# Routed experts: token rows scattered to their slots from SBUF and loaded back plainly, instead of stored in order and gathered

## The chip, the cores and the metric

The kernel runs on one core of one Trainium2 chip. A core has a matrix engine (TensorE, PE in the profile; PEld is its weight load), a vector engine (VectorE, DVE), a scalar engine (ScalarE, ACT), GpSimd (POOL) and SyncE (SP), which here only issues DMAs. The engines run their own instruction streams and wait for one another on semaphores. The metric is device time in microseconds (us), the median of several runs; lower is better.

## The reference, cut to what matters

The network takes x of shape (2, 1024, 128), two batches of 1024 tokens with 128 features, and has two blocks. The first (a recurrence and six layers of windowed attention with a gated feed-forward) is not touched by the change. The second is an attention with 16 heads over all tokens of a batch, and then a mixture of experts:

```python
h = _layernorm(x, axis=-1) * (1 + ca) + sa
x = x + ga * _L1_attn_ref(h, ...)                 # 16 heads of 64, relative bias, softmax
h = _layernorm(x, axis=-1) * (1 + cb) + sb
x = x + gb * _L1_ffn_ref(h, ...)

def _L1_ffn_ref(x, gate_w, w1, b1, w2, b2):       # E = 8 experts, F = 512
    router_logits = xf @ gate_w
    top_vals, top_idx = jax.lax.top_k(router_logits, 2)
    top_w = jax.nn.softmax(top_vals, axis=-1)
    onehot = jax.nn.one_hot(top_idx, E, dtype=xf.dtype)
    cw = jnp.einsum('tk,tke->te', top_w, onehot)
    out = jnp.zeros_like(xf)
    for e in range(E):
        h = jax.nn.gelu(xf @ w1[e] + b1[e], approximate=False)
        out = out + cw[:, e:e + 1] * (h @ w2[e] + b2[e])
```

Each token goes through two of the eight experts. Which two depends on the data, so the kernel sorts the 2048 (token, expert) pairs of a batch by expert on the chip and computes only those.

## The kernel before, in words

The second block starts at about 1650 us. Its attention (`attention`, L1283) runs over 128 tiles: 2 batches, 8 pairs of heads, 8 tiles of 128 queries. In each tile PE makes the scores (L1393), DVE their maxima (L1409), ACT the exponentials (L1419), DVE the reciprocal of their sum (L1422), and POOL scales the two probability tiles (L1423, "ap"). Two tiles later PE transposes them (L1432), ACT and DVE copy the transposes out of PSUM (L1435), and three tiles later PE multiplies them with the values (L1445). At tile 3 and 5 of each eight, PE makes the next pair's queries and keys (L1338, tiles "aq" and "ak") and values (L1359), SP loads two relative-bias tiles ("abias", L1377), and POOL subtracts their first column (L1381). The order of PE, DVE and ACT is the order in which the code calls them (`manual_schedule`); POOL's and SP's orders are left to a scheduler that works with its own estimates of time.

All the work on routing is cut into small pieces, kept in a list; after each tile one piece is taken from it (`next_piece`, L1279). When half a batch's attention is done (a segment of 512 tokens), `expert_tokens` (L1577) appends the pieces of its layer norm (`norm_pieces`), which centres the tokens (tile "ln_xc") and stores them in order to DRAM ("centred", L1496), and of its routing. When a batch is complete, `dispatch` (L1640) sorts its pairs. `summed` and `counted` make ranks by matmuls with a triangle of ones; `placed` gives each pair its slot (tile "slot": token by token, first and second choice) and each row its expert. A row is 128 slots that all have the same expert; there are ROWS = 2*8+8-1 = 23 rows a batch, 2944 slots, of which 2048 are filled. `split`, `hot0`, `hot1` and `listed` (32 matmuls, L1745) turn the map round, from slot to pair, and `numbered` makes of it "tokens" (which token a slot reads) and "homes" (where its result goes). Then `slots_gathered` (L1935) gathers each row's 128 tokens from "centred" with one indirect DMA on POOL, 23 a batch: for batch 0 within the attention of batch 1 (`first_rows`, two rows a piece), for batch 1 within the expert stage.

The expert stage (`experts`, L1857) runs 46 rows, one a step of a loop over n, with steps of different rows overlapped: `row_weights` (the row's expert is read into a register of SP, and 514 KB of weights are loaded, "row_w", L1954; 8 buffers, asked for up to 8 rows ahead, the first two rows' in the attention already), `row_features` of row n (PE turns the row, L1960, DVE scales it, L1962), `row_hidden` of row n-2 (8 matmul instructions, L1973, and four gelu on ACT, L1977), and `row_outputs` of row n-4 (8 matmul instructions, L1989, a product on DVE, "row_y", L1997, 12 buffers, and an indirect DMA on POOL that scatters the 128 results to "outputs" in DRAM, L1998). The late half of batch 1 (its last segment's layer norm and routing) has no attention left to lie beside: `late_steps` (L1888) hangs its parts on certain steps, `placed` and `split` on step 9, `numbered` on 13; from step 13 on one gather of batch 1 follows each step. From step 36 on the pairs of batch 0 are loaded ("pair_y", L2018; SP waits for all their scatters) and summed (L2034). Here PE, DVE, ACT and SP have a hand-made order, POOL the scheduler's.

Of the kernel before, what the change touches and what calls it, by code (L numbers as in the profile page):

```python
# [57 lines left out]

GATHER = 13
# [39 lines left out]
class Net:  # L99
# [1149 lines left out]
    def second_block(self):  # L1249
# [5 lines left out]
        engines = {ET.PE, ET.DVE, ET.Activation}  # L1255
        with ExitStack() as es:
# [7 lines left out]
            with ExitStack() as at:  # L1264
# [3 lines left out]
                with tc.manual_schedule(engines=engines):  # L1268
                    self.attention(work)
# [13 lines left out]
    def attention(self, work):  # L1283
# [10 lines left out]
        for n in range(len(tiles) + 3):  # L1294
# [75 lines left out]
    def relative_bias(self, head):  # L1370
# [91 lines left out]
    def norm_pieces(self, src, out, scale, bias, b, keep=None, home=None):  # L1462
# [16 lines left out]
        def centred():  # L1479
# [15 lines left out]
            if home is not None:  # L1495
                nc.sync.dma_start(out=home, in_=xc)  # L1496
# [32 lines left out]
    def dispatch_tables(self):  # L1529
# [43 lines left out]
        self.centred_rows = [home(f"centred{b}", [N, D]) for b in range(B)]  # L1573
        self.puts = [[], []]
        self.pair_rows = [home(f"outputs{b}", [2 * N + ROWS * 128, D]) for b in range(B)]

    def expert_tokens(self, seg):  # L1577
# [6 lines left out]
        rows = self.centred_rows[b][i * SEG : (i + 1) * SEG].rearrange("(i p) d -> p i d", p=128)  # L1584
# [5 lines left out]
        if seg == NSEG - 1:  # L1590
            self.late = self.late_norm(self.x3, h, b, tokens, rows), route
            return
        self.norm_pieces(self.x3, h, 4, 3, b, keep=tokens, home=rows)
# [10 lines left out]
    def late_norm(self, src, out, b, tokens, rows):  # L1604
# [19 lines left out]
        def centred():  # L1624
# [7 lines left out]
            nc.sync.dma_start(out=rows, in_=xc)  # L1632
# [7 lines left out]
    def dispatch(self, b):  # L1640
# [28 lines left out]
        def placed():  # L1669
# [28 lines left out]
            nc.vector.tensor_tensor(slot[:, 0], slot[:, 0], slot[:, 1], ALU.subtract)  # L1698
            end = get([128, E], "end")
# [12 lines left out]
            st["expert"] = expert  # L1712

# [39 lines left out]
        def numbered():  # L1753
            ps = st["list"][:, :ROWS]
            pair = get([128, ROWS], "pairs")
            nc.vector.tensor_scalar(pair, ps, -1.0, 0.0, ALU.add, ALU.max)
            second = get([128, ROWS], "second")
            nc.vector.tensor_scalar(second, pair, float(N), float(N), ALU.is_ge, ALU.mult)
            tokens = get([128, ROWS], f"tokens{b}", mybir.dt.uint32)
            nc.vector.tensor_tensor(tokens, pair, second, ALU.subtract)  # L1760
# [4 lines left out]
            self.plan[b] = st["expert"], tokens, homes  # L1765

        def shared():
# [14 lines left out]
            placed=placed,  # L1782
            split=split,
# [73 lines left out]
    def experts(self, work):  # L1857
# [11 lines left out]
        for n in range(len(order) + 4):  # L1869
            while loads < min(len(order), n + 8) and order[loads][0] in self.plan:  # L1870
# [17 lines left out]
    def late_steps(self, work, norm, route, slots):  # L1888
# [39 lines left out]
    def first_rows(self, j0):  # L1928

        for j in range(j0, min(j0 + 2, ROWS)):  # L1930
            self.gathered[0, j] = self.slots_gathered(self.disp, 0, j)
            if j < 2:
                self.early[j] = self.row_weights(self.disp, 0, j, 2)

    def slots_gathered(self, work, b, j, bufs=ROWS):  # L1935
# [208 lines left out]
```

## Time and profile before

| | us |
|---|---|
| median of 3 runs (2742.39 to 2746.73) | 2744.52 |
| the profiled execution, its own time | 2759.36 |
| its span, first to last instruction | 2757.6 |
| first block, until about | 1650 |
| attention of the second block | 1670 to 2602 |
| expert stage with its sums | 2602 to 2757 |

| stretch, us | PE busy | POOL busy | granted clock | GB/s of DMA |
|---|---|---|---|---|
| 2362.25 to 2415.30 (eight attention tiles) | 52.39 of 53.05 | 19.36 | 1.00 | 9 |
| 2285.24 to 2362.25 (eight tiles with batch 0's gathers) | 62.57 of 77.01 | 43.52 | 0.89 | 26 |
| 2652.15 to 2700.21 (rows 16 to 26) | 34.84 of 48.06 | 30.28 | 0.75 | 169 |
| 2700.21 to 2726.53 (rows 27 to 39) | 26.32 of 26.32 | 13.08 | 1.00 | 287 |

How to read the profile: a line of the timeline gives the start, the busy time, the engine, the line of the kernel, the operation, the tile written and the tiles read ("out<-in"), and how many instructions are merged; in brackets stands the idle time before it and what released it. "issue" there means that the engine waited for nothing that the profile shows, "remote" that the releaser could not be told. SPq is SP's issuing of a DMA, not its transfer. The ends of matmuls are modelled from their starts, so a busy PE need not be a PE at its peak. The granted clock is the share of the full clock that PE was given. For DMA_INDIRECT the time shown is the time that POOL takes to issue it.

### The profile page before, as it was taken

The page shows a single profiled execution, that of the slowest core. Times are in us where ns is not written, and L with a number is a line of the kernel's source. Part 1 is how long each engine was busy: PE and PEld are TensorE (multiplying, and loading weights), DVE is VectorE, ACT ScalarE, POOL GpSimd, SP SyncE. Part 2 cuts the span into 40 slices and gives each one's busy share as a digit, 9 for nine tenths or more (in the row PEclk, how much of TensorE's full clock was granted, in tenths as well). Part 3 has the DMA queues.
Part 4 walks back from the last instruction along what each step waited for, and adds up shares of the span by engine and source line. Part 5 has one row for each costly group of instructions (what it writes and reads, how often), then busy time and mean ns, then how long its engine had stood idle before and what let it go on. Part 6 is the DMA issues. An engine that isn't in the chain of part 4 may idle for free. (4 is left out here: it accounts for less than half of the span.)

```text
span 2757.6 us, 67119 instructions
## 1 busy us (share of the span) xinstructions
PE 2573.7 (93%) x29054; PEld 1735.0 (63%) x29054; DVE 1947.2 (71%) x2744; ACT 1726.1 (63%) x2562; POOL 1673.5 (61%) x1312
## 2 busy tenths in 40 slices
PE   7899999999999999999999989999999998999977
PEld 4466666666666666666666655666666665666676
DVE  6788788888878887878778845666665665666434
ACT  5467777777777777777777765555554553555424
POOL 3687888888888878887878733333332335333154
PEclk9999999999999999999999999999999999999979
DMA  7000100000010001000000010000000001000256
GB/s 193 4 2 2 32 2 9 25 10 2 9 32 2 7 4 32 2 9 2 2 2 2 2 43 18 7 7 11 9 7 11 11 7 43 8 1 1 74 165 219
DMA packets 44051, 71.02 MB, mean 26 GB/s; under 512 B 5511, under 2 KB 32269, under 8 KB 42733
## 3 DMA queue, kind: packets, MB, share of 16 engines
q1 hardware_dynamic: 40156, 59.24, 7.2%
q0 software_dynamic: 3168, 6.89, 0.9%
q8 instruction: 229, 3.75, 0.6%
q10 hardware_dynamic: 432, 0.61, 0.1%
q14 instruction: 66, 0.53, 0.1%
HBM read 61.56 MB, written 9.36 MB: 26 GB/s over the span
## 5 line engine op out<-in xcount | busy, mean ns | idle before, releaser
L1423 POOL TENSOR_SCALAR ap<-ap,a_den 128x1024 f32<-128x1024 f32 x256 | 287.0, 1134 | 557.7 <-DVE a_den L1422 557.6
L993 POOL TENSOR_TENSOR qk<-qk,turned 128x1024 f32<-128x1024 f32 x192 | 453.8, 2363 | 194.3 <-DVE turned L982 187.0
L1419 ACT ACTIVATE ap<-two,a_neg 128x1024 f32<-128x1024 f32 x256 | 285.4, 1115 | 295.7 <-DVE a_neg L1409 294.5
L1409 DVE TENSOR_REDUCE a_neg<-two 128x1 f32<-128x1024 f32 x256 | 301.2, 1218 | 175.9 <-PE two L1393 163.2
L1131 PEld LDWEIGHTS two<-px,wvo 128*128 128x128 f32 x3072 | 356.4, 192 | 56.8 <-issue 29.3
L956 PE MATMUL proj<-wqk,xs 128*128 128x512 f32 x764 | 370.4, 607 | 22.7 <-DVE turned L982 21.6
L1131 PE MATMUL two<-px,wvo 128*128 128x128 f32 x3072 | 361.6, 276 | 17.5 <-ACT xw L1093 17.2
L1005 POOL TENSOR_TENSOR qk<-qk,w_inv 128x1024 f32<-128x1024 f32 x192 | 361.6, 1904 | 3.9 <-ACT w_inv L1002 2.8
L1432 PEld LDWEIGHTS two<-fixed,ap 128*128 128x128 f32 x2048 | 223.1, 142 | 139.7 <-issue 121.2
L1432 PE MATMUL two<-fixed,ap 128*128 128x128 f32 x2048 | 277.3, 279 | 16.9 <-ACT ap L1419 14.1
L967 ACT ACTIVATE sq<-proj 128x1024 f32<-128x1024 f32 x191 | 195.9, 1026 | 133.7 <-PE proj L956 133.0
L1445 PE MATMUL two<-apT,av 128*64 128x128 f32 x4096 | 257.5, 279 | 15.5 <-ACT apT L1435 11.6
L975 DVE TENSOR_TENSOR qk<-proj,rot 128x1024 f32<-128x1024 f32 x191 | 232.6, 1218 | 49.1 <-ACT sq L967 43.4
L1393 PE MATMUL two<-ak,aq 64*128 64x512 f32 x1024 | 259.7, 615 | 4.7 <-DVE gates L1527 1.6
L1445 PEld LDWEIGHTS two<-apT,av 128*64 128x64 f32 x4096 | 225.4, 139 | 37.7 <-issue 21.3
L1079 POOL TENSOR_TENSOR p<-p,w_den 128x1024 f32<-128x1024 f32 x96 | 183.4, 1911 | 98.0 <-DVE ya L1141 86.0
L1121 ACT COPY px<-two 128x1024 f32<-128x1024 f32 x192 | 195.0, 1017 | 76.3 <-PE two L1112 76.3
L1027 PEld LDWEIGHTS two<-fixed,qk 128*128 128x128 f32 x1536 | 165.2, 141 | 111.1 <-issue 82.1
L982 DVE TENSOR_TENSOR turned<-proj,rot 128x1024 f32<-128x1024 f32 x191 | 231.9, 1214 | 1.5 <-POOL qk L993 1.5
L956 PEld LDWEIGHTS proj<-wqk,xs 128*128 128x128 f32 x764 | 133.0, 191 | 147.7 <-issue 110.7
L1027 PE MATMUL two<-fixed,qk 128*128 128x128 f32 x1536 | 204.4, 277 | 20.6 <-ACT px L1121 13.0
L990 DVE TENSOR_REDUCE w_ss<-sq 128x16 f32<-128x1024 f32 x192 | 221.3, 1192 | 1.5 <-ACT sq L967 1.5
(359 smaller groups left out, 4262.6 us busy)
## 6 DMA issues: line engine op xcount, KB each, us to landing
row_w<-expert_rows SPq DMA_DIRECT2D x46, 514.0 KB
wqk<-in_wqkv SPq DMA_DIRECT2D x6, 1024.0 KB
abias<-rel_turned SPq DMA_DIRECT2D x32, 192.0 KB
wv<-in_wqkv SPq DMA_DIRECT2D x6, 512.0 KB
wo<-in_wo SPq DMA_DIRECT2D x6, 512.0 KB
expert_rows<-in_ew SPq DMA_DIRECT2D x1, 2048.0 KB
expert_rows<-in_ew SPq DMA_DIRECT2D x8, 256.0 KB
pair_y<-outputs SPq DMA_DIRECT2D x16, 128.0 KB
```

The source lines that it names most:

```text
L956: self.nc.tensor.matmul(ps[:, g], x.step.xs[:, c0 : c0 + 128], x.step.weights[:, a, g * 512 : (g + 1) * 512], start=True, stop=True,)
L975: nc.vector.tensor_tensor(dst, ps.rearrange("p a (h d) -> p (a h) d", d=DH), cos.unsqueeze(1).to_broadcast([128, H, DH]), ALU.mult,)
L993: self.nc.gpsimd.tensor_tensor(x.qk[a], x.qk[a], x.turned.rearrange("p h e d -> p h (e d)"), ALU.add)
L1005: engine.tensor_tensor(x.qk[a], x.qk[a], x.inv[:, a].unsqueeze(2).to_broadcast([128, H, DH]), ALU.mult)
L1027: nc.tensor.transpose(ps[:, c // 4, c % 4 * 128 : (c % 4 + 1) * 128], flat[:, c * 128 : (c + 1) * 128], self.ident,)
L1131: nc.tensor.matmul(x.out[:, 0, :128].rearrange("p (b q) -> p b q", q=BLK), merged[:, c // 4, par, c % 4], x.px[:, :, h], start=(h == 0), s ...
L1393: nc.tensor.matmul(scores[par][:, j], q[r, tok], k[r, j * 512 : (j + 1) * 512], start=True, stop=True)
L1409: self.nc.vector.tensor_reduce(neg, ps, AX.XY, ALU.max, negate=True)
L1419: nc.scalar.activation(p, ps.rearrange("p a b -> p (a b)"), AF.Exp, bias=neg, accum_out=den)
L1423: nc.gpsimd.tensor_scalar(p, p, den, 1.0, ALU.mult, ALU.mult)
L1432: self.nc.tensor.transpose(ps[:, j // 4, j % 4 * 128 : (j % 4 + 1) * 128], p[:, j * 128 : (j + 1) * 128], self.ident)
L1445: nc.tensor.matmul(ops[r, :128], v[:, j, r], pT[par][:, j], start=(j == 0), stop=(j == NKT - 1))
```

## The change

The centred tokens are no longer stored in order. They stay in SBUF (`self.centred`), and once `placed` has given each pair its slot (copied to integers, "index"), POOL scatters them from there to "slot_rows" in DRAM, where a batch's 2944 slots lie in order: `sent(i)` is one indirect DMA of 128 tokens, 16 a batch, for the two choices of 8 tiles of tokens. For batch 0 they are 16 pieces, one after each attention tile; for batch 1 all 16 stand at step 9 of the expert stage. The slots that no pair fills must hold something finite, so both "slot_rows" are filled with zeros at the start of the second block, by one memset of 128x2944 on POOL and two stores.

The rows are then read with plain loads on SP (`rows_loaded`): all 23 of batch 0 in one, after the last piece of its `dispatch`; those of batch 1 in two, 6 and 17 rows, at step 21. A load waits for all sends of its batch, but the sends don't wait for one another (`put`, `after`). The three operations that made "tokens" in `numbered` go. `split` to `numbered` of batch 1 move from steps 9 to 13 to steps 11 to 15. POOL joins the engines whose order in the attention is given by hand; the subtraction of the bias columns, which its loader called so far, gets a place of its own (`biases_less`: after tile 1 for the first pair, after tile 6 of each eight for the next). "row_w" has 10 buffers instead of 8 and is asked for 6 rows ahead instead of 8, "row_y" 24 instead of 12.

```diff
-                with tc.manual_schedule(engines=engines):
+                with tc.manual_schedule(engines=engines | {ET.Pool}):
                     self.attention(work)
...
+            if n == 1:
+                self.biases_less(qk[0, 0])
+            if n < len(tiles) and t == 6 and n + NKT - t < len(tiles):
+                self.biases_less(qk[tiles[n + NKT - t][:2]])
...
-        r = self.get(self.att, [128, 3 * 128], "abiasr", bufs=4)
-        nc.gpsimd.tensor_tensor(r, t, t[:, 0:1].to_broadcast([128, 384]), ALU.subtract)
-        return r
+        return t
+
+    def biases_less(self, qk):
+        for i, t in enumerate(qk[2]):
+            r = self.get(self.att, [128, 3 * 128], "abiasr", bufs=4)
+            self.nc.gpsimd.tensor_tensor(r, t, t[:, 0:1].to_broadcast([128, 384]), ALU.subtract)
+            qk[2][i] = r
...
-                nc.sync.dma_start(out=home, in_=xc)
+                self.centred[home] = xc
...
-        self.centred_rows = [home(f"centred{b}", [N, D]) for b in range(B)]
-        self.puts = [[], []]
+        self.slot_rows = [home(f"slot_rows{b}", [ROWS * 128, D]) for b in range(B)]
+        zeros = self.disp.tile([128, ROWS, D], F32, tag="slots0_0", name="zeros", bufs=1)
+        nc.gpsimd.memset(zeros, 0.0)
+        for rows in self.slot_rows:
+            nc.sync.dma_start(
+                out=rows.rearrange("(j p) d -> p j d", p=128),
+                in_=zeros,
+            )
+        self.puts, self.sends, self.centred = [[], []], [[], []], {}
...
-            order = "summed counted placed split hot0 hot1 listed numbered shared".split()
-            self.pieces += [steps[k] for k in order]
-            self.pieces += [lambda j=j: self.first_rows(j) for j in range(0, ROWS, 2)]
+            self.pieces += [steps[k] for k in ("summed", "counted", "placed")]
+            self.pieces += [lambda i=i: steps["sent"](i) for i in range(2 * NKT)]
+            self.pieces += [steps[k] for k in "split hot0 hot1 listed numbered shared".split()]
+            self.pieces.append(self.first_rows)
...
-            nc.sync.dma_start(out=rows, in_=xc)
+            self.centred[b, PER_B - 1] = xc
...
+            index = st["index"] = get([128, 2, NKT], f"index{b}", mybir.dt.uint32)
+            nc.vector.tensor_copy(index, slot)
...
+        def sent(i):
+            c, t = i % 2, i // 2
+            put = nc.gpsimd.indirect_dma_start(
+                self.slot_rows[b],
+                bass.IndirectOffsetOnAxis(st["index"][:, c, t : t + 1], axis=0),
+                self.centred[b, t // TT][:, t % TT],
+                None,
+            )
+            self.put(self.sends[b], put)
...
-            while loads < min(len(order), n + 8) and order[loads][0] in self.plan:
+            while loads < min(len(order), n + 6) and order[loads][0] in self.plan:
...
-            j = n - GATHER
-            if 0 <= j < ROWS:
-                gathered[1, j] = self.slots_gathered(self.rows, 1, j, 20)
...
-        at(9, slots["placed"], slots["split"])
-        at(10, slots["hot0"])
-        at(11, slots["hot1"])
-        at(12, slots["listed"])
-        at(13, slots["numbered"])
+        at(9, slots["placed"], *(lambda i=i: slots["sent"](i) for i in range(2 * NKT)))
+        at(11, slots["split"])
+        at(12, slots["hot0"])
+        at(13, slots["hot1"])
+        at(14, slots["listed"])
+        at(15, slots["numbered"])
+        at(21, lambda: self.rows_loaded(work, 1, 0, 6), lambda: self.rows_loaded(work, 1, 6, ROWS))
...
-        x = self.get(work, [128, D], "slots", bufs=bufs)
-        self.nc.gpsimd.indirect_dma_start(
-            x, None, self.centred_rows[b], bass.IndirectOffsetOnAxis(self.plan[b][1][:, j : j + 1], axis=0)
-        )
-        return x
-
-    def row_weights(self, work, b, j, bufs=8):
+    def rows_loaded(self, pool, b, j0, j1):
+        self.n += 1
+        x = pool.tile([128, j1 - j0, D], F32, tag=f"slots{b}_{j0}", name=f"slots{self.n}", bufs=1)
+        rows = self.slot_rows[b][j0 * 128 : j1 * 128].rearrange("(j p) d -> p j d", p=128)
+        self.after(self.nc.sync.dma_start(out=x, in_=rows), self.sends[b])
+        for j in range(j0, j1):
+            self.gathered[b, j] = x[:, j - j0]
+
+    def put(self, earlier, put):
+        for other in earlier:
+            self.tc.declare_no_dep(put.ins, other.ins, reason="their places differ")
+        earlier.append(put)
+
+    def row_weights(self, work, b, j, bufs=10):
...
-        y = self.get(work, [128, D], "row_y", bufs=12)
+        y = self.get(work, [128, D], "row_y", bufs=24)
```

More of the change, by code (lines that the diff above doesn't have):

```diff
@@ L57 @@
 EW = 2 * F1 + F1 // 128
-GATHER = 13
 C_MG, C_MR, C_MK, C_MV, C_BG, C_BR, C_BK, C_BV, C_BO, C_W, C_U = range(11)
@@ L1583, in expert_tokens @@
         h = self.get(self.moe, [128, SEG], "mh", bufs=1)
-        rows = self.centred_rows[b][i * SEG : (i + 1) * SEG].rearrange("(i p) d -> p i d", p=128)
         if i == 0:
@@ L1590, in expert_tokens @@
         if seg == NSEG - 1:
-            self.late = self.late_norm(self.x3, h, b, tokens, rows), route
+            self.late = self.late_norm(self.x3, h, b, tokens), route
             return
-        self.norm_pieces(self.x3, h, 4, 3, b, keep=tokens, home=rows)
+        self.norm_pieces(self.x3, h, 4, 3, b, keep=tokens, home=(b, i))
         self.pieces += [route[k] for k in ("logits", "exponentials", "chosen", "weights")]
@@ L1599, in expert_tokens, with late_norm @@
             steps = self.dispatch(b)
-            order = "summed counted placed split hot0 hot1 listed numbered shared".split()
-            self.pieces += [steps[k] for k in order]
-            self.pieces += [lambda j=j: self.first_rows(j) for j in range(0, ROWS, 2)]
-    def late_norm(self, src, out, b, tokens, rows):
+            self.pieces += [steps[k] for k in ("summed", "counted", "placed")]
+            self.pieces += [lambda i=i: steps["sent"](i) for i in range(2 * NKT)]
+            self.pieces += [steps[k] for k in "split hot0 hot1 listed numbered shared".split()]
+            self.pieces.append(self.first_rows)
+    def late_norm(self, src, out, b, tokens):
         nc, mod, st = self.nc, self.mod1, {}
@@ L1754, in numbered @@
             ps = st["list"][:, :ROWS]
[L1755 to L1760, printed above, removed]
             spare = get([128, ROWS], "spares")
@@ L1764, in numbered @@
             nc.vector.scalar_tensor_tensor(homes, ps, -1.0, spare, ALU.add, ALU.add)
-            self.plan[b] = st["expert"], tokens, homes
+            self.plan[b] = st["expert"], homes
         def shared():
@@ L1782, in dispatch @@
             placed=placed,
+            sent=sent,
             split=split,
@@ L1926, in late_steps, with first_rows, after @@
         return steps
[L1928 to L1935, printed above, removed]
-        x = self.get(work, [128, D], "slots", bufs=bufs)
-        self.nc.gpsimd.indirect_dma_start(
-            x, None, self.centred_rows[b], bass.IndirectOffsetOnAxis(self.plan[b][1][:, j : j + 1], axis=0)
-        )
-        return x
-    def row_weights(self, work, b, j, bufs=8):
+    def first_rows(self):
+        self.rows_loaded(self.disp, 0, 0, ROWS)
+        for j in range(2):
+            self.early[j] = self.row_weights(self.disp, 0, j, 2)
+    def rows_loaded(self, pool, b, j0, j1):
[9 more added lines that the diff above has]
+        earlier.append(put)
+    def after(self, load, puts):
+        for put in puts:
+            self.tc.add_manual_dep(
+                load.ins,
+                put.ins.name,
+                mybir.DependencyInfo(mybir.DependencyClass.Sync, mybir.DependencyReason.DATA),
+                reason="reads what all put",
+            )
+    def row_weights(self, work, b, j, bufs=10):
         nc = self.nc
@@ L1995, in row_outputs @@
             )
-        y = self.get(work, [128, D], "row_y", bufs=12)
+        y = self.get(work, [128, D], "row_y", bufs=24)
         nc.vector.tensor_tensor(y, ps[:, :D], self.gates[:, b], ALU.mult)
         put = nc.gpsimd.indirect_dma_start(
-            self.pair_rows[b], bass.IndirectOffsetOnAxis(self.plan[b][2][:, j : j + 1], axis=0), y, None
+            self.pair_rows[b], bass.IndirectOffsetOnAxis(self.plan[b][1][:, j : j + 1], axis=0), y, None
         )
-        for other in self.puts[b]:
-            self.tc.declare_no_dep(put.ins, other.ins, reason="slots have homes of their own")
-        self.puts[b].append(put)
+        self.put(self.puts[b], put)
     def token_base(self, work, seg):
@@ L2017, in pairs_loaded @@
         rows = self.pair_rows[b][: 2 * N].rearrange("(c t p) d -> t p c d", c=2, p=128)
-        load = self.nc.sync.dma_start(out=y, in_=rows[t])
-        for put in self.puts[b]:
-            self.tc.add_manual_dep(
-                load.ins,
-                put.ins.name,
-                mybir.DependencyInfo(mybir.DependencyClass.Sync, mybir.DependencyReason.DATA),
-                reason="reads what all rows put",
-            )
+        self.after(self.nc.sync.dma_start(out=y, in_=rows[t]), self.puts[b])
         return y
```

## The prediction

> **What bounds the kernel now.** I read the busy table first: over the whole span TensorE (PE) is busy 93% and no other engine is near that, so only stretches where PE waits are worth anything. Then the granted clock in 40 slices, low in slice 39 alone, and the stretches of 10 us around the instructions that the diff removes, the gathers of line 1938. Columns after the stretch: its length, then PE, PE weight load, DVE, ACT, POOL busy, granted clock, DMA share, GB/s.
>
> ```profile
> PE 2573.7 (93%) x29054; PEld 1735.0 (63%) x29054; DVE 1947.2 (71%) x2744; ACT 1726.1 (63%) x2562; POOL 1673.5 (61%) x1312
> ...
> PEclk9999999999999999999999999999999999999979
> ```
>
> ```profile
> 2320.00:2330.00 10.00, 5.41 (x26) 2.66 (x24) 2.52 (x7) 1.02 (x1) 7.84 (x9) 0.97 0.23 53
> 2330.00:2340.00 10.00, 7.95 (x56) 6.12 (x56) 4.01 (x6) 3.35 (x5) 8.01 (x9) 0.69 0.17 40
> ...
> 2650.00:2660.00 10.00, 4.23 (x22) 3.65 (x22) 0.05 (x1) 1.14 (x4) 6.72 (x7) 0.69 0.35 105
> 2670.00:2680.00 10.00, 6.78 (x27) 5.93 (x27) 2.36 (x8) 3.05 (x12) 5.63 (x7) 0.54 0.44 120
> 2710.00:2720.00 10.00, 10.00 (x92) 10.00 (x91) 4.47 (x13) 5.71 (x20) 5.45 (x6) 1.00 0.88 294
> ```
>
> PE runs short for tens of us in these two places, and in both POOL issues gathers without a pause; with twice the DMA traffic and no gathers (2710) PE is full. So bandwidth isn't it. Next, the order of events in the first burst:
>
> ```profile
> 2310.09 2.22 POOL L1423 TENSOR_SCALAR ap<-ap,a_den 128x1024 f32<-128x1024 f32 x2 [7.22 <-DVE a_den L1422]
> 2312.84 1.08 POOL L1938 DMA_INDIRECT slots<-centred,tokens  x1 [0.53 <-DVE spares L1762]
> ...
> 2316.78 3.70 PE L1338 MATMUL two<-ah,aqkv 128*128 128x512 f32 x8
> ...
> 2322.84 1.02 ACT L1348 ACTIVATE aq<-two 128x1024 f32<-128x1024 f32 x1 [5.23 <-PE two L1432]
> ...
> 2324.28 1.23 DVE L1350 COPY ak<-two 128x1024 f32<-128x1024 f32 x1 [2.85 <-remote]
> ...
> 2329.10 2.23 POOL L1423 TENSOR_SCALAR ap<-ap,a_den 128x1024 f32<-128x1024 f32 x2
> ```
>
> Two harms are seen here. First, 13 gathers stand in one piece between two pairs of L1423, the scaling of probabilities that PE's transposes need: the pair ready at about 2317.8 starts at 2329.10. Second, PE itself is late: the eight matmuls of L1338 should end at 2320.5, their first half at 2318.6, yet ACT and DVE get them at 2322.84 and 2324.28. In the trace's semaphore records PE's updates come within 0.1 us of the modelled ends, except in these two bursts, where they are up to 4 us late; the lateness starts 1 to 2 us after the first gather has landed (2315.2 and 2648.9) and fades when none is landing. The plain loads and the scatters show none of it:
>
> ```profile
> 2725.29 0.97 POOL L1998 DMA_INDIRECT outputs<-row_y,homes  x1 [0.93 <-DVE row_y L1997]
> 2725.32 1.14 SPq L2018 DMA_DIRECT2D pair_y<-outputs  x2
> ...
> 2726.53 1.06 PE L1973 MATMUL hid<-row_h,row_w 128*128 128x128 f32 x8
> 2727.03 0.35 SPq L1954 DMA_DIRECT2D row_w<-expert_rows  x1
> 2727.42 1.06 PE L1989 MATMUL bank<-row_w,row_hid 128*128 128x128 f32 x8
> ```
>
> **The change part by part.** *Batch 0's gathers.* The eight tiles around them take 77.01 us (2285.24 to 2362.25, between two bias subtractions of L1381), the next eight 53.05. The first holds the 32 matmuls of L1745, 4.0 us, which stay. So gathers and POOL's order cost 77.0-53.05-4.0 = 20.0 us; if the two one-hot builds of 1.9 us also count, 16.2. I take 20.
>
> *Batch 0's sends.* Sixteen scatters replace them, one after each tile's L1423 pair. Nearest row: the scatter of L1998, 0.97 us and 0.30 of issue, 1.27. It stands where POOL idles 3.6 us before each pair ("3.64 <-DVE a_den"), so 0; without that cover 16x1.27 = 20. If a scatter delayed PE as a gather does (below, 0.94), 15. I take 0: L1998 is the same form, SBUF to DRAM through an index. No gain lies in them either.
>
> *Batch 0's load* of 2944 rows of 512 B: the 512-row store of L1496 took 1.03 us, 2.0 ns a row, so 5.9 us beside the attention. It is issued six pieces after the last send, so SP waits for nothing, and the bias loads behind it are wanted tiles later. Price for PE: 0 as beside pair_y, at most the gathers' own 20; I take 0.
>
> *Batch 1's gathers.* From row 16's first matmul (2652.15) to row 27's (2700.21) 48.06 us for 11 rows; a row in the clean stretch takes 8+8+1 matmuls, 1.90 us: 20.9. Of the 27.2 too much, 4.3 stand at rows 25 to 27, where the late softmax steps hold DVE and ACT; those stay. Row 16 itself is 1.3 late. So 27.2-4.3+1.3 = 24.2 goes; 20 if half of the rest is not the gathers', 28.5 if the 4.3 goes too. Per gather 43/46 = 0.94 us.
>
> *Batch 1's sends* go to POOL at step 9, behind six puts of L1998; the seventh and later puts queue behind all sixteen. DVE has the slots at about 2629.0 and copies them as an index in 0.2, so the sends end at 2629.2+16x1.27 = 2649.5 and have landed by 2652. Ten to eleven puts are then queued; 24 buffers of row_y hold them. POOL catches up at 1.27 a put against 1.90 a row, and row 22's put ends near 2671.5, while SP asks for batch 0's pairs at step 36, near 2689. PE's price as above: 0, at most 15.
>
> *The new wait.* At step 21 SP waits for the sends, then loads 6 and 17 rows of slots; row_w loads queue behind it, but they now run in 10 buffers and are about 8 rows (15 us) early, so nothing there is late. SP comes to it once row 26's weights are asked for, which waits for row 16's outputs: without stalls row 16's hidden matmuls are at 2650.8 and its outputs end at about 2656.5, after the sends. The first load: 1.0 to the first packet, 768x2.0 ns = 1.5, and 1.3 to 2.5 for the 514 KB of row_w ahead of it: there at 2660.3 to 2661.5. PE turns that row two steps later, 2660.3. I take 1 us; bounds 0 and 3.
>
> Rules to weigh here. The Trainium skill's "DMA: Bandwidth & Descriptors", Anatomy of one DMA, gives a fixed 2.0 us plus bytes/436e3: an estimate of 2.9 us for 393 KB where the row gives 2.5, so 0.4 us more, a sum of 42.6 instead of 43.0. Against the change speaks "TensorE: Matmul & The Clock Gate", Part 1: one idle window of about 3.4 us halves PE's clock; a wait of that size would cost more than itself. The trace agrees (0.5 granted after the stalls); by the rule the 3 us bound above just escapes it.
>
> *The rest.* The memset of 128x2944: L1423's 1.12 us for 1024 columns gives 3.2 us, 1.8 to 5.8 by the small iotas and memsets; POOL idles 4.4 us there before its first pair, and no longer does four bias subtractions before that; 0, at most 1.4. The two zero stores, 5888 rows, 12 us by the row above, run beside the first tiles: 0. The moved bias subtractions (2x0.8) stand after a pair with 2 us of slack, as now. DVE gains two index copies of 0.2 and loses six small operations: 0. Removed stores of centred: 0, SP is idle.
>
> Sum: 20+24.2-1 = 43 us. The profiled execution took 2759.36 around a span of 2757.6, 14.8 above the median, so it should read about 2716 (span 2714.5), and the median 2744.5-43 = 2701.5.
>
> **The rivals.** *Only attention gains (density).* PE is late because POOL writes descriptors without pause, and sixteen sends with the puts behind them do the same. For it: the bursts are POOL's densest stretches. Against: gathers issued from 2679.8 on, but landing only at 2684, left PE on time till then. Then 2744.5-20 = 2725.
>
> *The slots come late.* Each send takes twice as long, 2.5 us: the last lands near 2671, the slots at 2675, PE stands 14 us and restarts at half clock (1.48 and 1.71 for 0.89 and 0.89, two rows, 3 us): 43-16 = 27 less, 2718. Against: three puts in a row, 1.27 us apart from 2737.6, and each landed in time.
>
> *Slower: the sends run one after another,* each waiting for its receipt. It decides when the slots come 43+5.5 us after 2660: 16 sends in 75 us, 4.7 us each; at 5.5 us each it gives 2762. For it: they share a target, and a semaphore per eighth DMA can hold the next. Against: puts share a target too, and land 1.6 to 2.5 us after their issue.
>
> *No change:* PE is late through 512-byte pieces arriving in SBUF, whoever sends them; the plain loads bring as many bytes, 2744. Against: pair_y above.
>
> **How the numbers follow.** Forecast 0.72 (own range 2690 to 2713, from 20, 16.2, 24.2+-4, 0 to 3), density 0.10, late slots 0.09, no change 0.04, slower 0.05. The range 2690 to 2727 takes in the first three but for their tails. No change from what a measurement can tell is 0.2%, 5.5 us: faster 0.91, same 0.03, slower 0.06.
>
> **What would show it.** Right: no stretch of 10 us in 2310 to 2350 with PE under 8; eight tiles there in about 57 us; rows at 1.9 us from row 16 on with the clock at 1.00; ACT and DVE on time behind PE. Wrong: PE semaphores late after the sends (density); DVE's row_h waiting for slots at row 23 (late slots); POOL sends spaced over 2 us; the attention's plain periods above 53 us, which nothing here provides for.

## The result, and the profile after

| | median, us | range | ratio to before, 95% interval |
|---|---|---|---|
| before | 2743.15 | 2732.42 to 2746.73 | |
| after | 2720.70 | 2718.36 to 2723.07 | 0.9928 [0.9906, 0.9949] |
| forecast | 2701.5 | 2690 to 2727 | 0.9843 |

The change gains 22 us (14 to 26 by the interval) where 43 were forecast. The profiled execution of after took 2722.42 (span 2720.6), an ordinary one. That of before, on which the sum was built, took 2759.36: more than any execution of before beside which the medians were taken. Profile against profile the gain is 36.9 us; median against median it is 22.4. That gap is the main thing to explain.

The busy table and the granted clock of the page of after:

```profile
PE 2562.5 (94%) x29054; PEld 1725.8 (63%) x29054; DVE 1949.1 (72%) x2740; ACT 1725.5 (63%) x2562; POOL 1661.7 (61%) x1299
...
PEclk9899999999999999999999998999999999999999
```

PE's busy time fell by 11 us with the same 29054 matmuls, and the granted clock rose from 0.984 to 0.988 of full speed over the span. Then the stretches of 10 us, with the columns of the forecast's table:

```profile
2310.00:2320.00 10.00, 10.00 (x98) 6.83 (x94) 6.33 (x11) 6.52 (x10) 5.22 (x5) 1.00 0.05 15
2320.00:2330.00 10.00, 10.00 (x71) 6.18 (x70) 5.56 (x8) 4.37 (x6) 4.52 (x5) 1.00 0.04 14
2330.00:2340.00 10.00, 10.00 (x109) 7.92 (x107) 7.39 (x12) 5.69 (x9) 4.15 (x4) 1.00 0.03 8
...
2640.00:2650.00 10.00, 9.51 (x86) 9.31 (x84) 4.66 (x14) 6.06 (x22) 7.56 (x9) 1.00 0.89 300
2650.00:2660.00 10.00, 7.46 (x52) 7.50 (x53) 1.92 (x7) 3.71 (x10) 7.57 (x8) 0.83 1.04 357
```

The hole at 2310 to 2350 is closed. The one at 2650 is smaller, and a new thing stands in it, the wait for batch 1's slots. In the timeline:

```profile
2646.82 1.31 SPq L1961 DMA_DIRECT2D slots<-slot_rows  x2
...
2647.56 1.06 PE L2011 MATMUL hid<-row_h,row_w 128*128 128x128 f32 x8
2652.54 0.30 PE L1998 MATMUL bank<-fixed,slots 128*128 128x128 f32 x1 [3.03 <-DMA slots<-slot_rows]
2652.67 1.93 PE L2011 MATMUL hid<-row_h,row_w 128*128 128x128 f32 x8
```

The load is issued at 2646.8 and lands 5.6 us later, PE stands 3.03 us, and the next eight matmuls take 1.93 instead of 1.06, at half clock (the granted clock from 2652.78 to 2656.20 is 0.50). In attention the sends look as forecast, one behind each pair of scalings, in POOL's slack:

```profile
2318.03 2.21 POOL L1430 TENSOR_SCALAR ap<-ap,a_den 128x1024 f32<-128x1024 f32 x2 [2.44 <-DVE a_den L1429]
...
2320.41 1.03 POOL L1734 DMA_INDIRECT slot_rows<-ln_xc,index  x1 [0.17 <-issue]
...
2323.89 2.21 POOL L1430 TENSOR_SCALAR ap<-ap,a_den 128x1024 f32<-128x1024 f32 x2 [2.45 <-DVE a_den L1429]
```

The two profiles, by part (starts of the scalings and of each row's first hidden matmul; a second profile of before, from the first experiment, beside them):

| us | before | before, again | after |
|---|---|---|---|
| first scaling of attention at | 1674.1 | 1683.1 | 1683.7 |
| first to last scaling | 906.8 | 905.6 | 891.8 |
| row 0 to row 45, hidden matmuls | 135.5 | 110.2 | 106.5 |
| from there to the end | 18.5 | 18.5 | 17.6 |
| end of the span | 2757.6 | 2741.7 | 2720.6 |

The first line is scatter that the change does not touch: over all profiles of this study the first scaling starts between 1674 and 1685. The third line holds the answer: the 25 us between the two profiles of before are the excess of rows 16 to 27 (48.06 us in the first, 22.5 in the second), which the forecast booked as a gain.

### The profile page after: what moved, and what is told of

It is laid out like the page before. It is cut to its first block, busy times and chain, and to the rows that moved or that the text cites. A ratio compares the mean times of both kernels' runs of the same rounds, so it can differ in the third digit from the quotient of the medians.

```text
span 2720.6 us, 67041 instructions
## 1 busy us (share of the span) xinstructions
PE 2562.5 (94%) x29054; PEld 1725.8 (63%) x29054; DVE 1949.1 (72%) x2740; ACT 1725.5 (63%) x2562; POOL 1661.7 (61%) x1299
## 5 line engine op out<-in xcount | busy, mean ns | idle before, releaser
L954 PE MATMUL proj<-wqk,xs 128*128 128x512 f32 x764 | 370.7, 608 | 22.4 <-DVE turned L980 21.2
```

The source lines that it names most:

```text
L954: self.nc.tensor.matmul(ps[:, g], x.step.xs[:, c0 : c0 + 128], x.step.weights[:, a, g * 512 : (g + 1) * 512], start=True, stop=True,)
```

## The experiments

Late updates of PE, below, are counted as in the forecast: semaphore updates over 0.3 us behind the modelled end of their matmul. Ratios are to the kernel before on the same chip. The runs fell on five chips, on each of them in one stretch of time only, so "chip" below stands for the chip or the moment; the runs do not separate the two.

**The kernel before, again.** No edit.

> The kernel before, unchanged, to see how far two of its executions differ. If the gathers' harm is fixed by the program, the profile again shows 77 us for the eight attention tiles of batch 0's gathers and 48 us from row 16 to row 27, the time again lies near 2759 when profiled, and the other executions lie within about 5 us of each other. If the harm differs from execution to execution (the theory made after the result: the profiled execution of before was 15 us above its median and 27 us above its fastest, 2732.42), the times spread over more than 10 us, and a profile nearer to 2740 shows that much less excess in just these two stretches: together about 27 us of excess where the first profile had 24.0 and 27.2, with the plain tiles at 53.0 and the plain rows at 1.90 as before.

2741.40 us, ratio 0.9997 [0.9983, 1.0012]; twelve executions from 2730.4 to 2748.3. Rows 16 to 24 take 1.90 us each while the same 23 gathers are issued and land, and of PE's updates none is late, there or in attention. The stretches where the forecast's profile had PE at 4.23 and 6.78:

```profile
2650.00:2660.00 10.00, 10.00 (x81) 10.00 (x80) 4.11 (x15) 5.11 (x19) 5.29 (x6) 0.87 0.58 165
2660.00:2670.00 10.00, 10.00 (x92) 10.00 (x91) 4.82 (x16) 6.22 (x23) 7.59 (x8) 1.00 0.89 321
2670.00:2680.00 10.00, 10.00 (x92) 9.91 (x91) 4.91 (x22) 8.43 (x25) 7.71 (x8) 1.00 0.95 320
```

But the eight attention tiles still take 76.0 us, with PE on time. So the forecast's two harms come apart: the place of the gathers in POOL's order is always there, PE's lateness is not.

```profile
2322.25 2.21 POOL L1423 TENSOR_SCALAR ap<-ap,a_den 128x1024 f32<-128x1024 f32 x2 [10.51 <-DVE a_den L1422]
2324.99 1.08 POOL L1938 DMA_INDIRECT slots<-centred,tokens  x1 [0.53 <-DVE spares L1762]
...
2340.24 0.95 POOL L1938 DMA_INDIRECT slots<-centred,tokens  x1 [0.30 <-issue]
2341.22 2.23 POOL L1423 TENSOR_SCALAR ap<-ap,a_den 128x1024 f32<-128x1024 f32 x2
```

Thirteen gathers stand between two pairs: 16.8 us from the end of the one pair to the start of the next.

**The hand order alone.**

```diff
-                with tc.manual_schedule(engines=engines):
+                with tc.manual_schedule(engines=engines | {ET.Pool}):
...
+            if n == 1:
+                self.biases_less(qk[0, 0])
+            if n < len(tiles) and t == 6 and n + NKT - t < len(tiles):
+                self.biases_less(qk[tiles[n + NKT - t][:2]])
```

> The kernel before with GpSimd's order in attention given by hand and the bias subtractions moved as in the change, all else as before: the gathers of batch 0 stay, two after each tile's pair of L1423 instead of up to 13 in one piece. If the block of gathers in front of a pair was the harm (order), the eight tiles fall from 77 to about 57 us and the time by up to 20 us, to about 2724. If the landing gathers make PE late whatever stands between them (the forecast's second harm), the same number of gathers costs the same over more tiles: 2743 within 8 us, with late PE in twelve tiles instead of eight.

2730.84, ratio 0.9962 [0.9946, 0.9978]. Attention takes 891.7 us, as in after (891.8), with all gathers still in it:

```profile
2334.93 2.21 POOL L1431 TENSOR_SCALAR ap<-ap,a_den 128x1024 f32<-128x1024 f32 x2 [7.13 <-DVE a_den L1430]
2337.30 1.08 POOL L1946 DMA_INDIRECT slots<-centred,tokens  x1 [0.16 <-issue]
2338.68 0.97 POOL L1946 DMA_INDIRECT slots<-centred,tokens  x1 [0.30 <-issue]
2340.79 2.22 POOL L1431 TENSOR_SCALAR ap<-ap,a_den 128x1024 f32<-128x1024 f32 x2 [1.14 <-DVE a_den L1430]
```

Two gathers fit into the slack. All that the change gains in attention is the order. The time falls by less than these 13.9 us, 2740.39 to 2730.84 beside each other: the rows take 112.5 us, 2.3 more than before (rows 9 to 14 take 23.8 instead of 20.5).

**One batch sent, the other gathered.** Both are the changed kernel; the gathered batch stores its centred tokens and uses the old gathers, in the hand order. Where batch 1 is gathered (send0), its list steps also stand at their old places, steps 9 to 13.

```diff
+SENT = (True, False)      # send0;  (False, True) in send1
...
+            if SENT[0]:
                 self.pieces += [lambda i=i: steps["sent"](i) for i in range(2 * NKT)]
...
+            if not SENT[1] and 0 <= j < ROWS:
+                gathered[1, j] = self.slots_gathered(self.rows, 1, j, 20)
```

> The changed kernel with batch 0 sent and loaded, but batch 1 gathered as before (23 gathers from row 13 on). By the two profiles attention gained 15 us and the expert rows 29; if the medians share the gain of 22.5 us in that proportion, batch 0 is worth 7.6 us and this reads about 2735; by the forecast's own sizes it would be 20 of 43, and 2724. Density (sends harm as gathers do) has no gain from either batch but from the order, and gives the time of the hand order alone.

> The changed kernel with batch 1 sent and loaded, but batch 0 gathered, two gathers after each tile's pair of scalings. By the proportion of the two profiles batch 1 is worth 14.8 of the 22.5 us: about 2728; by the forecast's sizes 23 of 43: 2720. Rows 16 to 45 at 1.90 us but for the wait for the first slots (4.9 us beyond two plain rows), and attention with PE late behind the gathers.

send0: 2727.51, ratio 0.9948 [0.9930, 0.9965]; attention 891.6, rows 110.3. send1: 2716.32, ratio 0.9908 [0.9888, 0.9928]; attention 891.6, rows 106.5. So batch 0's sends are worth nothing in attention, and sending batch 1, with its list steps at their new places, brings the rows' 3.8 us. (send1's median is 4.4 us under after's; the intervals of the two ratios overlap, and no window of the two profiles accounts for it.)

**The same burst again, of gathers and of sends.** In the hand order, batch 0's gathers go out as 13 and 10; in the changed kernel, its sixteen sends in one piece.

```diff
-            self.pieces += [lambda j=j: self.first_rows(j) for j in range(0, ROWS, 2)]
+            self.pieces += [lambda j=j: self.first_rows(j) for j in range(0, ROWS, 13)]
```
```diff
-            self.pieces += [lambda i=i: steps["sent"](i) for i in range(2 * NKT)]
+            self.pieces.append(lambda: self.burst(steps["sent"]))
```

> The hand-ordered kernel with batch 0's 23 gathers put out as 13 and 10 in one piece each, as GpSimd had them before, instead of two after each pair. If what the change gained in attention is the order alone, the first piece, 13 x 1.26 = 16.4 us less about 3 us of slack, comes back once: attention from first to last scaling 891.7 -> about 905 us, as in both profiles of before (906.8 and 905.6), with all of PE's updates on time; the time about 13 us above the hand order. If something else of before's attention was slow (the bias subtractions' place), attention stays at 892.

> The changed kernel with batch 0's sixteen sends in one piece between two pairs of scalings (a memset of one column between them) instead of one after each pair. By the order theory the kind of transfer does not matter: 16 x 1.4 = 22 us of GpSimd less 3 to 4 us of slack, so attention 891.8 -> 906 to 910 us and the time 14 to 18 us above the changed kernel's, about what the changed kernel gained in all. By the forecast (only gathers harm, sends are hidden beside the attention's slack) the block would still be seen, but PE's updates would tell them apart: late behind gathers, on time behind sends; in the runs so far they are on time behind both.

hand_burst: 2741.28, ratio 0.9993 [0.9979, 1.0006]; attention 909.5 (+17.8), its eight tiles 77.7 against 59.9. burst_sends: 2733.36, ratio 0.9956 [0.9939, 0.9972]; attention 904.0 (+12.2). No update of PE is late in either. The block in front of a pair costs, whatever kind of transfer it holds; with the gathers it takes away all that the hand order gave.

**The slots loaded earlier.**

```diff
-        at(21, lambda: self.rows_loaded(work, 1, 0, 6), lambda: self.rows_loaded(work, 1, 6, ROWS))
+        at(19, lambda: self.rows_loaded(work, 1, 0, 3))
+        at(20, lambda: self.rows_loaded(work, 1, 3, ROWS))
```

> The changed kernel with batch 1's slots loaded in 3 and 20 rows at steps 19 and 20 instead of 6 and 17 at step 21. In the changed kernel SP comes to the load at 2646.8, about 2 us after the sends have landed, and it takes 5.6 us; PE stands 3.0 us at 2649.5 and then runs two rows at half clock: 4.9 us beyond plain rows. If the place and size of the load set this, rows 20 to 23 go to 1.90 and the time falls by 4 to 5 us, to 0.991 of before (2716). If the landing is bound by the sends and a transfer's fixed time, SP waits for the sends at 2645, the three rows land at 2649 to 2650, and 0 to 2 us of the wait stay.

> Batch 0 gathered in the hand order, batch 1 sent, with the earlier load: the same with the part of the change left out that gained nothing in attention (891.6 us with gathers as with sends). If batch 0's sends are worth nothing, this and the changed kernel with the early load agree within 3 us; if the 4 us between the medians of the two with the late load (2716.3 and 2720.7) are real, it is 4 us faster, about 2712.

early: 2723.35, ratio 0.9920 [0.9904, 0.9937]; send1_early: 2717.03, ratio 0.9906 [0.9886, 0.9926]. Rows 20 to 22 run in 2.0 us, but the wait comes back at row 26, for the twenty rows of the second load:

```profile
2647.98 0.71 SPq L1962 DMA_DIRECT2D slots<-slot_rows  x1
...
2658.78 0.30 PE L1999 MATMUL bank<-fixed,slots 128*128 128x128 f32 x1 [3.62 <-DMA slots<-slot_rows]
```

2560 pieces of 512 bytes land 10.7 us after their issue, behind the weights in front of them. The wait moved. Row 0 to row 45 takes 107.4 us in early and 103.6 in send1_early, against 106.5 in both with the late load, and neither ratio is clear of the one with the late load.

**After, three loads, and the steps alone, on a third chip.** Two more edits: the slots in three loads, and before's hand order with the list steps of batch 1 at the changed kernel's places, but gathers.

```diff
+        at(19, lambda: self.rows_loaded(work, 1, 0, 3), lambda: self.rows_loaded(work, 1, 3, 8))
+        at(21, lambda: self.rows_loaded(work, 1, 8, ROWS))
```
```diff
-        at(9, slots["placed"], slots["split"])
+        at(9, slots["placed"])
+        at(11, slots["split"])
...
+        at(15, slots["numbered"])
```

> The changed kernel, unchanged, beside the others on the same chip. If its gain over before is as first measured, ratio 0.9928, it reads about 20 us under before, 4 us above the kernel with batch 1 sent alone (0.9908). If the 4 us were the draw of the executions, its ratio is 0.991 too. Its profile: attention 891.7 us, row 0 to row 45 106.5 us with the wait of 4.9 us at rows 20 to 22, PE's updates on time.

> The changed kernel with batch 1's slots loaded in three parts: rows 0 to 2 and 3 to 7 at step 19, rows 8 to 22 at step 21. With two parts of 3 and 20 rows the wait went from row 23 to row 26 (3.6 us), since the second part took about 8 us; five rows land earlier by 15 x 128 pieces of 512 bytes. If the amount of the part in front is what is waited for, rows 20 to 25 run within 1 us of plain, row 0 to row 45 falls from 106.5 to about 102.5 us and the time by 4 us; if the transfers share one rate of about 2 to 3 ns a piece, what is put off comes back at row 31, and the sum stays at 106.

> Batch 0 gathered in the hand order, batch 1 sent and loaded in three parts: 4 us under the same kernel with one late load (0.9908 of before), so about 0.9893, if the wait goes; the same 0.9906 if it only moves.

> The kernel before with the hand order, and with the steps of batch 1's slot list at the changed kernel's places (split at 11 to numbered at 15, gathers from step 15 on) but still gathered. In the changed kernel rows 9 to 20 took 26.3 us where before took 30.0. If the places of DVE's steps gave that, they do so here: rows 9 to 20 in 26 us, and the late pair loads (rows 40 to 45, 3 to 5 us too long behind GpSimd's queue of gathers and puts) stay or grow by two rows, for a time of 2727 to 2731, 0 to 4 us under the hand order. If the sends gave it, rows 9 to 20 stay at 30 us.

| third chip | median, us | ratio | row 0 to 45 | late updates |
|---|---|---|---|---|
| before | 2765.39 | | | |
| after_again | 2737.62 | 0.9897 [0.9876, 0.9917] | 123.5 | 58 |
| loads3 | 2736.37 | 0.9892 [0.9872, 0.9911] | 116.8 | 61 |
| send1_loads3 | 2736.79 | 0.9880 [0.9860, 0.9900] | 118.9 | 58 |
| hand_steps | 2746.48 | 0.9926 [0.9908, 0.9944] | 131.7 | 77 |

Here the changed kernel takes 17 us longer than at first, and before 25 us longer than on the first chip of the experiments (2761.79 to 2773.59, where 59 executions elsewhere lay between 2730.4 and 2751.3). It looks like the lateness of the forecast's profile, and the changed kernel has it too: rows 12 to 15 take 11.3, 8.0, 7.5 and 3.2 us, just while its sixteen sends go out (2619.0 to 2640.3). Stretches of after_again:

```profile
2620.00:2630.00 10.00, 8.39 (x67) 7.81 (x66) 5.93 (x16) 2.61 (x10) 7.56 (x9) 0.99 0.58 191
2630.00:2640.00 10.00, 8.04 (x29) 6.61 (x29) 1.15 (x3) 1.14 (x4) 7.87 (x8) 0.50 0.48 158
2640.00:2650.00 10.00, 6.26 (x20) 4.51 (x20) 0.94 (x5) 0.84 (x4) 5.20 (x7) 0.50 0.13 39
2650.00:2660.00 10.00, 10.00 (x76) 10.00 (x76) 5.37 (x14) 5.73 (x22) 5.13 (x5) 0.82 0.83 260
```

and how it begins: the hidden matmuls should end at 2625.1, and ACT gets them at 2626.98; the outputs should end at 2626.0, and DVE gets them at 2629.12.

```profile
2624.04 1.06 PE L2011 MATMUL hid<-row_h,row_w 128*128 128x128 f32 x8
2624.23 0.97 POOL L1734 DMA_INDIRECT slot_rows<-ln_xc,index  x1 [0.30 <-issue]
...
2624.93 1.06 PE L2027 MATMUL bank<-row_w,row_hid 128*128 128x128 f32 x8
...
2626.98 1.14 ACT L2015 ACTIVATE row_hid<-hid,row_w 128x128 f32<-128x128 f32 x4 [3.98 <-issue]
...
2629.12 0.29 DVE L2035 TENSOR_TENSOR row_y<-bank,gates 128x128 f32<-128x128 f32 x1 [2.66 <-remote]
```

hand_steps settles a smaller point: rows 9 to 14, ahead of its late rows, take 16.6 us, as in after (16.8), where before took 20.5 and hand 23.8. So that gain came from the places of DVE's steps, not from the sends.

**Bursts of both kinds, by themselves.** Twelve gathers behind tile 12's scalings and twelve scatters behind tile 28's are added to the changed kernel; their data is not used.

```diff
+            for i in range(12):
+                rows = bass.IndirectOffsetOnAxis(numbers[:, i : i + 1], axis=0)
+                if n == 12:
+                    nc.gpsimd.indirect_dma_start(self.zeros[:, i], None, self.slot_rows[1], rows)
+                if n == 28:
+                    put = nc.gpsimd.indirect_dma_start(scratch, rows, self.earlier, None)
```

> The changed kernel with two bursts added in tiles of attention that run at 53.0 us per eight: twelve gathers in one piece behind the scalings of tile 12, twelve scatters in one piece behind those of tile 28 (each with a memset of one column), of rows that nothing needs. If only GpSimd's occupation costs, each burst takes the same from its eight tiles: 12 x 1.4 = 16.8 us less about 3 of slack, 13 to 14 us, and the time is 26 to 28 us above the changed kernel's. If gathers also make PE late and scatters do not (the forecast), the gather burst costs more by up to 0.94 x 12 = 11 us and its PE updates come over 0.3 us late; if both do on a chip where PE is late at all (as in the four runs on the chip where the kernel before took 2765 us), both bursts show late updates.

2761.27, ratio 0.9962 [0.9948, 0.9976], on a fourth chip, where before took 2769.88 (2764.65 to 2780.34). The tiles' 53.0 become 65.2 with the gathers and 64.1 with the scatters: 12.2 and 11.1 us. PE is late behind both, by 17.2 and 16.2 us summed. First the gather burst, then the scatter burst; the matmuls of L1376 make values that ACT copies:

```profile
1764.16 1.09 POOL L1321 DMA_INDIRECT zeros<-slot_rows,numbers_u  x1 [0.16 <-issue]
...
1766.82 2.05 PE L1376 MATMUL two<-aqkv,ah 128*128 128x128 f32 x16
...
1778.55 1.01 ACT L1384 COPY av<-two 128x1024 f32<-128x1024 f32 x1 [10.89 <-remote]
```
```profile
1882.50 1.09 POOL L1323 DMA_INDIRECT scratch<-earlier,numbers_u  x1 [0.17 <-issue]
...
1885.15 2.05 PE L1376 MATMUL two<-aqkv,ah 128*128 128x128 f32 x16
...
1896.14 1.01 ACT L1384 COPY av<-two 128x1024 f32<-128x1024 f32 x1 [10.15 <-remote]
```

Matmuls that should end at 1768.9 and 1887.2 reach ACT 9.7 and 8.9 us later. PE itself goes on at first: after the gathers' L1376 its next matmuls start at 1768.71 and 1769.68, before ACT has the result. On this chip gathers and scatters do the same to PE. Here it lies under POOL's own block: the bursts cost no more than the 13 to 14 us expected of POOL's time alone. In the expert rows no such cover exists.

**After and three loads, twice more.** On the fourth chip and on a fifth (before 2773.82).

> The changed kernel once more, beside the two versions with three loads. Where PE's updates are on time: ratio about 0.992, row 0 to row 45 106.5 us. Where they are late as in its last run: 0.990, with 15 to 17 us more in the rows behind the sixteen sends.

> The changed kernel with batch 1's slots in three loads. In its first run rows 20 to 25 ran plain, but 15 us were lost at rows 16 to 18 to late updates of PE. Where updates are on time the whole wait of 4.9 us should be gone: row 0 to row 45 about 102 us, 4 to 5 us under the changed kernel. If the wait was only covered by the late rows ahead of it, it comes back and the rows take 106.

> Batch 0 gathered in the hand order, batch 1 sent, three loads. If batch 0's sends and zero fill cost 4 us that no window shows (2716.3 against 2720.7, 2717.0 against 2723.4), this is about 4 us under the changed kernel with three loads; if they cost nothing, the two agree within 2 us.

> The changed kernel beside the one with three loads, once more. On a chip where PE's updates are on time (before near 2742): about 2721, rows 0 to 45 in 106.5 us, late updates none. On one where they are late (before near 2767): about 2737, with 16 to 17 us more in the rows behind the sixteen sends.

> The changed kernel with batch 1's slots in three loads. Where PE is on time, rows 20 to 25 at 1.90 but for the late softmax steps, rows 0 to 45 in about 102 us and the time 4 to 5 us under the changed kernel's; if the second load only moves the wait, as with two loads (3.6 us at row 26), 106 us and no gain. Where PE is late the rows behind the sends hide the wait as in its two runs so far, and 1 to 6 us are gained.

| chip | after | three loads | batch 1 alone sent, three loads |
|---|---|---|---|
| fourth | 2736.95, 0.9878 [0.9859, 0.9897] | 2730.99, 0.9866 [0.9845, 0.9887] | 2732.63, 0.9865 [0.9845, 0.9884] |
| fifth | 2737.22, 0.9862 [0.9845, 0.9879] | 2735.05, 0.9860 [0.9843, 0.9876] | |

Both chips show late updates in every kernel run there; rows 0 to 45 take 122.7 us in after_b and 123.0 in after_c. After_b shows a second side of the lateness, where PE itself starts late. Its 32 list matmuls (L1773) lie from 2626.1 to 2647.0, 20.9 us, where after takes 3.9; PE stands between them for nothing that the profile shows:

```profile
PE bank L1773 <- issue: 13.9, 20, 1.5
```
```profile
2641.81 0.39 PE L1773 MATMUL bank<-ids,onehot 128*128 128x23 f32 x1 [1.22 <-issue]
2643.25 0.20 PE L1773 MATMUL bank<-ids,onehot 128*128 128x23 f32 x1 [1.05 <-issue]
2644.66 0.63 PE L1773 MATMUL bank<-ids,onehot 128*128 128x23 f32 x3 [1.21 <-issue]
2646.78 0.20 PE L1773 MATMUL bank<-ids,onehot 128*128 128x23 f32 x1 [1.50 <-issue]
```

The first of these lines (from the view of waits) is 13.9 us in total, 20 times, 1.5 us the longest; they are most of the 16.2 that after_b's rows lose. In after_c PE still waits for its slots, in loads3_c it no longer does, and rows 20 to 24 take 1.9 each. The waits of PE in the expert stage of after_c:

```profile
PE hid L2011 <- issue: 3.8, 6, 1.3
PE bank L1998 <- DMA slots<-slot_rows: 3.3, 1, 3.3
```

and of loads3_c, where the line of the slots is gone:

```profile
PE hid L2012 <- issue: 4.1, 5, 1.7
PE bank L1773 <- issue: 2.5, 4, 1.0
PE bank L2028 <- issue: 2.5, 4, 1.1
PE bank L2028 <- ACT row_hid L2016: 2.4, 1, 2.4
```

Three loads were 1.3, 6.0 and 2.2 us under after in the three pairs by the medians, some 1.4, 3.3 and 0.6 by the ratios. The intervals overlap, so the wait is shown to be gone, and a gain of 1 to 3 us in the time is likely rather than shown. Of the versions with both batches sent, the one with three loads is the one to keep; with batch 1 alone sent it is as fast (0.9880 against 0.9892, 0.9865 against 0.9866). Neither was run where PE is on time. There send1 and send1_early, with batch 0 gathered in the hand order, had the lowest times, and on the chips with late PE they had no lead.

## Why the prediction was right and wrong

**Batch 1's gathers, 24.2 us: the step that failed.** The excess of rows 16 to 27 was real in that profile and absent in the next one of the same program, with the same gathers (110.2 against 135.5 us). It belongs to the chip (or the moment) and not to the kernel's time where the medians were taken: by the count used above the forecast's profile has 101 late updates, the second one none. Of the 4.3 us that were to stay at rows 25 to 27, 1.6 stay there. The forecast saw that its execution stood 14.8 us above the median and carried its gains over undiminished; by the second profile those 14.8 us were part of the very excess that it counted. On the three chips that show late updates the change is worth more, 27.8, 32.9 and 36.6 us by the medians. But even there the rows would not have gained 24.2: row 0 to row 45 takes 122.7 to 123.5 us after the change, against 135.5 in the forecast's profile, since the sends bring a lateness of their own.

**Sends at nothing for PE.** Where PE is on time this holds. Where it is late, sixteen sends cost 123.5-106.5 = 17.0 us (16.2 and 16.5 in the other two profiles of after), 1.0 us each; 23 gathers cost 135.5-110.2 = 25.3, 1.1 each. It is about one price for both kinds, near the bound of 15 that the forecast named and set to 0. (Its 0.94 a transfer divided the net 43 by 46 gathers; with the 44.2 of the gathers it is 0.96.) That the scatters showed none of it was misread: in the forecast's own profile 20 of PE's updates between 2703 and 2742, where POOL issues puts alone, are 0.3 to 0.7 us late. The rival "density" said what the late chips show, that sends harm as gathers do; its reason, the writing of descriptors, no run tests. Its 2725 lies near the 2720.7 measured, but by accident, since PE was on time there. The argument made against it, gathers issued from 2679.8 that did not yet harm PE, weighed too much. The rival "late slots" is near too, at 2718, and has the place, row 23, but neither the size nor the cause: PE stood 3.03 us, not 14, and the sends went at 1.27 us, not 2.5.

**Batch 0's gathers, 20 us.** The cause was right in its first half, POOL's block, and the second, PE's lateness, adds 1 us at most (77.0 against 76.0 for the eight tiles). POOL's order, and it alone, gives 13.9 us (905.6 to 891.7, with no sends at all). The rest of the 20 stays: the tiles with the list steps still take 61.0 and 59.9 us under the hand order, 2.1 more than before in the one and 2.9 more than plain tiles and the 4.0 of the list matmuls in the other. Of the bounds given, 16.2 was the nearer.

**The new wait, 1 us.** 4.9: 3.03 of standing and 1.9 of half clock, where the bounds were 0 and 3. The place was right, and so was the sends' pace of 1.27 us. The load took 5.6 us instead of 3.8 to 5.0, and the half clock behind the stop was not added, though the forecast named its price for another rival. The Trainium skill, "TensorE: Matmul & The Clock Gate", Part 1, gives about 3.4 us without work as the window (its figure) that halves the clock; here 3.03 us were enough, so a wait under that figure isn't safe. By "DMA: Bandwidth & Descriptors", Anatomy of one DMA, a fit for DMAs issued by GpSimd, an estimate for the load is 2.9 us; it took 5.6, issued by SP, behind 514 KB of weights and in pieces of 512 bytes.

**What nothing in the forecast provided for** is worth 8.6 us in the rows (profile of after against the second one of before). 3.72 come from rows 9 to 19, where the list steps lie further apart. 4.84 come from rows 25 to 45. There, in before, gathers and puts took 2.5 us of POOL a row against 1.90, batch 0's last puts were late, so its pairs were loaded late, and DVE waited for them with the next row's features queued behind it. In the second profile of before:

```profile
2713.14 1.39 DVE L2034 SCALAR_TENSOR_TENSOR macc<-pair_y,share,macc 128x128 f32<-128x128 f32 x4 [4.11 <-DMA pair_y<-outputs]
...
2714.91 1.16 PE L1973 MATMUL hid<-row_h,row_w 128*128 128x128 f32 x8 [2.31 <-DVE row_h L1962]
```

With sixteen sends in place of 23 gathers POOL has caught up by 2667, and these waits are gone. The larger row_y and row_w buffers were never run alone; send0, which has them and still gathers batch 1, takes 44.3 us for rows 25 to 45, against 45.9 before and 41.0 after, so they can explain only the smaller part. The forecast worked out that queue for after and not for before.

**The sum, where PE is on time:** attention 13.8, rows 3.72+4.84-4.91 = 3.7, the end 0.9: 18.4 us, inside the 14 to 26 measured. (The spans of the two profiles differ by 21.1; the rest lies between the last scaling and row 0, 24.2 us against 21.0, where other profiles of after take 22.6 and 24.2, and before the first scaling.) Memset, zero stores, batch 0's load, index copies: 0, as forecast; the plain tiles stay at 53.0.

## What to carry to other kernels

A profile that lies well above the median tells first how it differs from an ordinary execution; before its excess is booked as a gain, it needs a second execution, or the sum must be scaled to the median. When a change bundles an engine's order with a new data path, run the order alone: here it gave all of attention's gain. A transfer that removes a stall brings a wait of its own; price the landing behind what is queued ahead of it, and the half clock after it.

## What the runs showed of the hardware that was not expected

PE's updates come late on some chips and not on others, with the same program. On two chips no profile of any kernel shows one over 0.3 us late (four and four profiles). On three chips every profile does (four, four and two), 49 to 77 of some 2170: the large ones, several us each, where POOL issues sends or gathers without a pause, and ones of about 0.5 us in the rows after. Single sends behind each tile, and two gathers behind each tile, leave PE's updates in attention on time there too, but for two of them. The large ones go with about 1 us per transfer in the expert rows.

It is not PE's updates alone. On the three chips 29 to 43 of ACT's 2039 updates and 27 to 36 of DVE's some 2460 are over 0.3 us late as well, on the two others 0 to 3. And between matmuls of one line PE stands, with no semaphore to wait for, 4.3 to 13.5 us a profile on the three chips, and on the two others not once for over 0.15 us. Small latenesses may be of the record: an update is taken to be the next one recorded, and on the three chips 53 to 84 of PE's have no record of their own. The large ones are real, since engines stand idle for them: ACT up to 16.0 us and DVE up to 13.9 in after_again.

What makes the difference stays open: the runs cannot choose a chip, each chip was seen in one stretch of time, and that the forecast's profile came from such a chip is inferred from its time, its rows and its late updates, not recorded.
